# Attention and expert layer on one core: exponentials turned by way of HBM instead of on TensorE, scores ahead of values, and the order of the last scatters

## The chip, the cores and the metric

The kernel runs on one core of one Trainium2 chip. The core has TensorE (PE in the profile; its weight loads are PEld), VectorE (DVE), ScalarE (ACT), GpSimd (POOL) and SyncE (SP), which work through queues of their own and wait for one another by semaphores. Transfers are issued from the queues of SP, ACT and POOL and are carried by 16 DMA engines. The metric is device time of one execution in microseconds, the median of several. All data is float32.

## What is computed

Eight sequences of 512 tokens with 256 features go through one pre-norm layer: causal attention with one head, and a mixture of eight experts (two per token) beside a shared expert. Cut to what matters:

```
x = x + attention(layernorm(x))          # softmax(q k^T / 16, causal) v
h = layernorm(x)
shared = (silu(h @ sg.T) * (h @ su.T)) @ sd.T
p = sigmoid(h @ router.T + bias);  top 2 of 8, weights normalised to sum 1
routed = sum over the two experts e of weight * ((silu(h @ g[e]) * (h @ u[e])) @ d[e])
out = x + shared + routed
```

## The kernel before

**Tiling.** A tile has 128 partitions. A sequence has NT = 4 row blocks of 128 tokens; features are ND = 2 chunks of 128; the hidden layer has NI = 4 chunks. The weights of q and k are folded into one matrix (`w_qk`), so the scores are (x w_qk) x^T and only q is projected.

**Stages.** First a loop over sequences (`for b in range(B)`, L576): attention, router, the scatter of normalised tokens into rows by expert (`rows_h` in HBM), and half of the shared expert of an earlier sequence at a time. Then the routed experts in tiles of 256 or 128 rows (L821, results scattered to `rows_y`), and last the sums with the remaining shared work.

**One turn of the loop.** For each row block i, `scores` (L394) multiplies q by x^T (L399), adds the causal mask (L403), takes the row maximum (L405) and writes the exponentials to `ex` (L408). `attend` (L415) has PE transpose the i+1 squares of `ex` against an identity (L419), ScalarE copy them from PSUM to `exT` (L421), and PE multiply by the values (L426); VectorE adds the result to x (L429, the *residual sum* `summed`), takes mean and variance (L163, L164), GpSimd raises the variance to -1/2 (`rstd`, L170), and VectorE normalises to `hn` (L316). The scores of the next row block are issued ahead of the current block's values. During the last row block, q of the next sequence is projected (`project_q`, L375); then come its first scores and its values (`project_v`, L387, copied by VectorE at L391).

**Turning by way of HBM.** Normalised x of the sequences from 2 on and half of `hn` already go another way: SP writes them to HBM (L355), four transfers read them back so that each 32 partitions hold what a 32x32 transpose needs (L359), and VectorE transposes blocks of 32x32 (L364). The other half of `hn` is transposed on PE (L331).

**The rest of a turn.** `chosen` (L649) yields the transposes, the router product (L445), and the choice of two experts on VectorE, which ends in `run`, running counts by expert (L485). `places_of` (L490) turns counts into row numbers `at` with two small matmuls (L494, L495); it is called as `placed()` halfway through the shared expert's down product (`midway`, L546). `shared_beside` (L514) does the gate/up products (L528), the hidden product (L541, L544, marked `hid`) and the down product (L551). `dispatch` (L507) scatters a row block of `hn` with two indirect transfers on GpSimd (L509), spread over the row blocks of the next turn (L636).

**Order.** Instructions are written in program order, and a scheduler fixes each engine's queue at build time, taking what it reckons ready first. `tc.issue_after(x)` puts the instructions of a block behind x in the queue of x's own engine, and of that engine alone. `marks` keeps instructions for this. A pool's `bufs` is the number of buffers for a name; a writer waits until the oldest is free. PSUM has four buffers for scores, values and gate/up (`ps_m`), two for attention and down products (`ps_o`).

**The expert tiles.** How many single tiles are needed depends on the tokens. Tiles up to `SURE` are unconditional (L821), later ones are nested in conditions on a count read at run time (`go_on`, L844).

Of the kernel before, what the change touches and what calls it, by code (L numbers as in the profile page):

```python
# [26 lines left out]
def kernel(  # L27
# [37 lines left out]
    SURE = MEAN - 2  # L65
# [10 lines left out]
    VIA = [b for b in range(1, B) if b != B - 2]  # L76
    RS = 1.0 / D ** 0.5
# [15 lines left out]
    hn_d = {b: dram.tile([S // 2, D], F32, tag=f"hnd{b}", name=f"hnd{b}") for b in VIA}  # L93
    xn_d = {b: dram.tile([S, D], F32, tag=f"xnd{b}", name=f"xnd{b}") for b in range(2, B)}
# [172 lines left out]
    with ExitStack() as first, ExitStack() as inner:  # L267
# [66 lines left out]
        def first_norm(xb, step=NT):  # L334
            mv = small.tile([P, NT, 2], F32, tag="mv", name="mv")
            rstd = small.tile([P, NT], F32, tag="rstd", name="rstd")
            for c in range(NT):
                stats_of(mv, xb[:, c, :], c)
                if c % step == step - 1:
                    rstd_of(rstd[:, c + 1 - step : c + 1], mv[:, c + 1 - step : c + 1, :])  # L340
            rows = work.tile([P, NT, D], F32, tag="xn", name="xn")
# [9 lines left out]
        def sent_to_blocks(via, rows):  # L351
# [6 lines left out]
            for a in range(P // Q):  # L358
                nc.sync.dma_start(out=blocks[ts(a, Q)], in_=via[:, ts(a, L)].rearrange("(s i) l -> i s l", i=Q))  # L359
            return blocks  # L360
# [21 lines left out]
        def project_v(xT):  # L382
            v = work.tile([P, NT, D], F32, tag="v", name="v")
            for c in range(NT):
# [6 lines left out]
                nc.vector.tensor_copy(v[:, c, :], pm)  # L391
            return v

        def scores(i, qT, xT):  # L394
# [11 lines left out]
            ex = work.tile([P, S], F32, tag="ex", name="ex")  # L406
            tot = small.tile([P, 1], F32, tag="tot", name="tot")
            nc.scalar.activation(ex[:, :n], sc[:, :n], AF.Exp, bias=top, accum_out=tot)  # L408
# [6 lines left out]
        def attend(xb, i, ex, inv, v, mv, rstd, hn, meanwhile=None):  # L415
            n = (i + 1) * P
            pt = ps_t.tile([P, S], F32, tag="t", name="pt")
            for j in range(i + 1):
                nc.tensor.transpose(pt[:, ts(j, P)], ex[:, ts(j, P)], ident)  # L419
            exT = work.tile([P, S], F32, tag="exT", name="exT")  # L420
            marks["exT"] = nc.scalar.copy(exT[:, :n], pt[:, :n]).ins  # L421
# [3 lines left out]
            for j in range(i + 1):  # L425
# [3 lines left out]
            summed = nc.vector.scalar_tensor_tensor(  # L429
                out=xb[:, i, :], in0=av, scalar=inv, in1=xb[:, i, :], op0=ALU.mult, op1=ALU.add  # L430
            )
# [58 lines left out]
        def places_of(b, mask):  # L490
# [8 lines left out]
            for r in range(TOP):  # L499
# [4 lines left out]
                nc.vector.tensor_copy(at[:, r, :], slot)  # L504
# [9 lines left out]
        def shared_beside(b, half, hT, midway=None, early=None, steps=(), halfway=None):  # L514
# [8 lines left out]
            for m in range(NI):  # L523
# [20 lines left out]
                marks["hid"] = nc.vector.tensor_tensor(out=hid[:, m, :], in0=pg[:, 1, :], in1=sg, op=ALU.mult).ins  # L544
            for j in range(n // P):
# [15 lines left out]
        rows, normed = first_norm(xb, step=1)  # L561
# [13 lines left out]
        sc, sent, to_send, placed = scores(0, qT, xT), None, [], None  # L575
        for b in range(B):  # L576
            xb, ahead_T = total[b], None
            if b == 0:
                with tc.issue_after(normed):
                    rows, normed = first_norm(total[1])  # L580
                    ahead_T = turned_by_array(rows)
                with tc.issue_after(normed):
                    rows, _ = first_norm(total[2])
                blocks[2] = sent_to_blocks(xn_d[2], rows)
            elif b + 1 < B:
                ahead_T = work.tile([P, ND, S], F32, tag="xT", name="xT")
                turn_squares(ahead_T, blocks[b + 1], 0)
# [3 lines left out]
            if b and b + 2 < B:  # L591
                with tc.issue_after(marks["run"]):
                    rows, _ = first_norm(total[b + 2])
                blocks[b + 2] = sent_to_blocks(xn_d[b + 2], rows)
# [9 lines left out]
            for i in range(NT):  # L604


                if i + 1 < NT:
                    with nullcontext() if i or not b else tc.issue_after(marks["routed"]):
                        ahead = scores(i + 1, qT, xT)
                elif b + 1 < B:  # L610
# [3 lines left out]
                    xb, i, *sc, v, mv, rstd, hn, rest if i == NT - 1 and ahead_T is not None else None  # L614
                )
                sc = ahead
                if b in VIA and i == NT // 2:
                    halves = sent_to_blocks(hn_d[b], hn[:, : NT // 2, :D])
                if i == 0 and b + 1 in blocks:
# [379 lines left out]
```

## Time and profile before

| | us |
|---|---|
| median of 3 runs | 692.43 (691.06 to 693.13) |
| profiled execution | 694.9 |
| its span | 693.1 |
| PE busy | 675.8 |
| VectorE busy | 299.7 |
| ScalarE busy | 155.1 |
| GpSimd busy | 159.2 |
| one turn of the loop (109.53 to 138.78) | 29.25 |

The span runs from the first to the last instruction of the profiled execution; the execution's own time has 1.8 us around it. In the span the loop over sequences ends at about 257, routed experts begin at 277, and the closing sums at 628. Matmul ends are modelled, and a matmul of float32 appears as two records. In rows with an arrow, what stands left of it is written and what stands right is read; xN is the number of instructions; after a bar stand busy time and the mean of one in ns. A bracket in a timeline gives the idle time before an instruction and what ended it.

### The profile page before, as it was taken

The numbers are of one execution on the slowest core, as the hardware profiler recorded it, in microseconds if no ns is written. First come the engines' busy times: TensorE is split into PE (matmuls) and PEld (weight loads), VectorE is DVE, ScalarE is ACT, GpSimd is POOL, SyncE is SP. The second block draws the span as 40 slices with busy tenths as digits, with TensorE's granted clock in tenths as the row PEclk, the third lists the DMA queues.
The fourth block names the chain that finished last, engine by engine and source line by source line (L and its number), as shares of the span: only waits on it lengthen the run. The fifth ranks groups of instructions, "written<-read, shape, count | busy, mean of one in ns | idle before, by whom it ended". The sixth has DMA issues, their size and how long they took to land.

```text
span 693.1 us, 10478 instructions
## 1 busy us (share of the span) xinstructions
PE 675.8 (98%) x3258; PEld 550.6 (79%) x3258; DVE 299.7 (43%) x1009; ACT 155.1 (22%) x364; POOL 159.2 (23%) x210
## 2 busy tenths in 40 slices
PE   6999999999999799999999999999999999998998
PEld 5687776878777678888888888888888899994556
DVE  4667768677686565212212211222222112222665
ACT  2423233232333212221111111111111112111120
POOL 3106153351523540012112112112112111121000
PEclk9999999999999999999999999999999999999999
DMA  7775052241501263976555445435534447823875
GB/s 231 214 262 168 29 141 75 79 130 54 183 21 71 92 180 62 314 214 204 167 156 174 160 123 175 161 122 175 164 111 166 155 156 205 260 96 130 246 232 176
DMA packets 112794, 108.00 MB, mean 156 GB/s; under 512 B 72448, under 2 KB 92800, under 8 KB 112736
## 3 DMA queue, kind: packets, MB, share of 16 engines
q1 hardware_dynamic: 93536, 46.51, 24.9%
q10 hardware_dynamic: 12912, 43.53, 18.5%
q0 software_dynamic: 6288, 17.24, 7.0%
q8 instruction: 29, 0.48, 0.3%
q14 instruction: 29, 0.24, 0.1%
HBM read 77.55 MB, written 29.70 MB: 155 GB/s over the span
## 4 chain that ended last, share of the span: by engine, by line
PE 95%; DVE 3%; issue 1%; DMA 1%; ACT 1%; POOL 0%; SPq 0%; ACTq 0%
PE pg L771 17%; PE pu L771 17%; PE po L794 17%; PE pg L528 9%; PE av L426 5%; PE sc L399 5%; PE po L551 5%; PE pm L387 4%; PE pm L375 3%; PE pg L882 3%; PE po L941 3%; PE pu L882 3%; PE pt L419 1%; PE lT L445 1%; PE pt L331 1%
## 5 line engine op out<-in xcount | busy, mean ns | idle before, releaser
L757 DVE TENSOR_TENSOR hidp<-pu,sgt 128x512 f32<-128x512 f32 x56 | 38.6, 690 | 207.6 <-PE pu L771 192.1
L800 POOL DMA_INDIRECT rows_y<-y,to x56 | 53.5, 955 | 271.0 <-ACT y L799 147.3
L771 PE MATMUL pg<-hTt,w 128*128 128x256 f32 x448 | 105.9, 379 | 0.0
L771 PE MATMUL pu<-hTt,w 128*128 128x256 f32 x448 | 105.8, 379 | 0.0
L794 PE MATMUL po<-w_down,hidp 128*128 x448 | 101.3, 379 | 0.0
L771 PEld LDWEIGHTS pg<-hTt,w 128*128 128x128 f32 x448 | 85.0, 190 | 11.7 <-ACT sgt L756 0.2
L771 PEld LDWEIGHTS pu<-hTt,w 128*128 128x128 f32 x448 | 85.1, 190 | 11.6
L794 PEld LDWEIGHTS po<-w_down,hidp 128*128 128x128 f32 x448 | 85.0, 190 | 11.5
L528 PE MATMUL pg<-hT,w_sh 128*128 128x256 f32 x320 | 74.6, 382 | 0.2 <-ACT hT L332 0.2
L509 POOL DMA_INDIRECT rows_h<-hn,at x64 | 64.7, 1010 | 25.1 <-issue 16.1
L756 ACT ACTIVATE sgt<-pg 128x512 f32<-128x512 f32 x67 | 39.9, 597 | 122.2 <-PE pg L771 115.7
L528 PEld LDWEIGHTS pg<-hT,w_sh 128*128 128x128 f32 x320 | 58.9, 190 | 9.3 <-issue 1.4
L799 ACT COPY y<-po 128x256 f32<-128x256 f32 x67 | 24.9, 372 | 157.8 <-PE po L794 94.7
L170 POOL TENSOR_TENSOR rstd<-var,minus_half 128x1 f32<-128x1 f32 (+1 forms) x43 | 27.6, 645 | 136.2 <-DVE var L169 135.1
L399 PE MATMUL sc<-xT,qT 128*128 128x128 f32 (+3 forms) x128 | 42.8, 438 | 0.0
L426 PEld LDWEIGHTS av<-v,exT 128*128 128x128 f32 x160 | 29.1, 189 | 16.3 <-ACT exT L421 8.5
L426 PE MATMUL av<-v,exT 128*128 128x256 f32 x160 | 40.8, 386 | 0.0
L551 PE MATMUL po<-w_sh,hid 128*128 128x256 f32 x160 | 38.7, 380 | 2.1 <-DVE first L220 1.3
L551 PEld LDWEIGHTS po<-w_sh,hid 128*128 128x128 f32 x160 | 30.0, 190 | 7.1 <-DVE first L220 1.7
L375 PE MATMUL pm<-xT,w_qk 128*128 128x512 f32 x64 | 31.1, 593 | 0.0
L163 DVE BATCH_NORM_STATS2 bnst<-total 128x6 f32<-128x256 f32 x64 | 26.2, 412 | 7.5 <-DMA total<-in_x_dram 7.5
L387 PE MATMUL pm<-wv_sb,xT 128*128 128x256 f32 x128 | 29.1, 380 | 0.2 <-ACT xT L332 0.2
(150 smaller groups left out, 749.6 us busy)
## 6 DMA issues: line engine op xcount, KB each, us to landing
w<-in_gate_w_dram ACTq DMA_DIRECT2D x41, 512.0 KB
w<-in_up_w_dram ACTq DMA_DIRECT2D x41, 512.0 KB
yl<-rows_y SPq DMA_DIRECT2D x32, 256.0 KB
h<-rows_h SPq DMA_DIRECT2D x112, 64.0 KB
w_down<-in_down_w_dram SPq DMA_DIRECT2D x8, 512.0 KB
out_dram<-total SPq DMA_DIRECT2D x32, 128.0 KB
total<-in_x_dram SPq DMA_DIRECT2D x7, 512.0 KB
xnd<-xn SPq DMA_DIRECT2D x6, 512.0 KB
```

The lines of the kernel that those rows point to most:

```text
L375: nc.tensor.matmul(pm, lhsT=w_qk[:, k, ts(m, P)], rhs=xT[:, k, :], start=(k == 0), stop=(k == ND - 1),)
L387: nc.tensor.matmul(pm, lhsT=xT[:, k, ts(c, P)], rhs=wv_sb[:, k, :], start=(k == 0), stop=(k == ND - 1),)
L399: nc.tensor.matmul(sc[:, :n], lhsT=qT[:, k, ts(i, P)], rhs=xT[:, k, :n], start=(k == 0), stop=(k == ND - 1),)
L426: mixed = nc.tensor.matmul(av, lhsT=exT[:, ts(j, P)], rhs=v[:, j, :], start=(j == 0), stop=(j == i))
L509: lands(nc.gpsimd.indirect_dma_start(out=rows_h[:, :], out_offset=bass.IndirectOffsetOnAxis(ap=at[:, r, c : c + 1], axis=0), in_=hn[:, c, ...
L528: mm = nc.tensor.matmul(pg[:, w, :], lhsT=w_sh[:, ds(w * gu + k * I + m * P, P)], rhs=hT[:, k, at], start=(k == 0), stop=(k == ND - 1),)
L551: nc.tensor.matmul(po, lhsT=hid[:, m, ts(j, P)], rhs=w_sh[:, ds(2 * gu + m * D, D)], start=(m == 0), stop=(m == NI - 1),)
L756: nc.scalar.activation(sg, pg, AF.Silu)
L771: nc.tensor.matmul(dst[:, m, :], lhsT=w[:, i, k, ts(m0 + m, P)], rhs=hT[:, ts(k, n * P)], start=(k == 0), stop=(k == ND - 1),)
L794: nc.tensor.matmul(po, lhsT=hid[:, m, ts(j, P)], rhs=w_down[:, ds(w + m * D, D)], start=(m == 0), stop=(m == NI - 1),)
L800: nc.gpsimd.indirect_dma_start(out=rows_y[:, :], out_offset=bass.IndirectOffsetOnAxis(ap=to[:, j : j + 1], axis=0), in_=y, in_offset=None,)
L882: nc.tensor.matmul(dst, lhsT=w_sh[:, ds(off + k * I + m * P, P)], rhs=hT[:, k, :], start=(k == 0), stop=(k == ND - 1),)
```

## The change

For sequences 1 to 6 (`SENT`) the exponentials are no longer transposed on PE. All four row blocks' scores are computed together at the end of the turn before, ahead of the values. The exponentials of row blocks 0 to 2 stand side by side in one tile of 6 squares, those of row block 3 in one of 4. Each tile is written to HBM and read back by four transfers in runs of 32 elements (128 bytes), and VectorE turns it with one block transpose behind the hidden product (`behind`). `attend` then takes its part of the turned tile. Sequences 0 and 7 keep the transposes on PE.

With it: the values are copied by ScalarE for those sequences; `first_norm` is split into statistics (`first_stats`, at the end of the turn) and normalisation (`midway`), for sequence b+3 in turn b where it was b+2; q of the next sequence is projected in two halves, before row blocks 0 and 2; the shared result is added (`added`) at the turn's end; loads of x and down weights, and the write of `hT`, queue behind the new gathers on SP; `placed()` on VectorE stands behind the new transposes. In the last sequence, row block 2 dispatches one pair of scatters instead of two, and row block 3 the other three. `SURE` grows by one, so one more expert tile is unconditional.

```diff
-    SURE = MEAN - 2
+    SURE = MEAN - 1
+    SENT = range(1, B - 1)
+    BLOCKS = NT * (NT - 1) // 2, NT
...
-        def first_norm(xb, step=NT):
+        def first_stats(xb, step=NT):
             mv = small.tile([P, NT, 2], F32, tag="mv", name="mv")
...
+            return xb, mv, rstd
+
+        def first_norm(xb, mv, rstd):
             rows = work.tile([P, NT, D], F32, tag="xn", name="xn")
...
-        def project_v(xT):
+        def project_v(xT, copy=nc.vector.tensor_copy):
...
-                nc.vector.tensor_copy(v[:, c, :], pm)
+                copy(v[:, c, :], pm)
...
+        def part(of, i):
+            return of[1] if i == NT - 1 else of[0][:, ds(i * (i + 1) // 2 * P, (i + 1) * P)]
+
+        def sent_to_squares(via, ex):
+            if "blocks" in marks:
+                with tc.issue_after(marks["blocks"]):
+                    nc.sync.dma_start(out=via, in_=ex)
+            else:
+                nc.sync.dma_start(out=via, in_=ex)
+            n = via.shape[1] // P
+            blocks = work.tile([P, n * P], F32, tag=f"squares{n}", name="squares", bufs=1)
+            for a in range(P // Q):
+                marks["sent"] = nc.sync.dma_start(
+                    out=blocks[ts(a, Q)].rearrange("j (t s i) -> j t s i", t=n, i=Q),
+                    in_=via[:, :].rearrange("(s j) (t a i) -> a j t s i", j=Q, t=n, i=Q)[a],
+                ).ins
+            return blocks
+
+        def turn_exponentials(blocks):
+            exT = []
+            for of in blocks:
+                exT.append(work.tile(list(of.shape), F32, tag=f"exTs{of.shape[1]}", name="exTs", bufs=1))
+                marks["turned"] = nc.vector.transpose(out=exT[-1], in_=of).ins
+            return exT
+
-        def scores(i, qT, xT):
+        def scores(i, qT, xT, into=None):
...
-            ex = work.tile([P, S], F32, tag="ex", name="ex")
+            ex = work.tile([P, S], F32, tag="ex", name="ex")[:, :n] if into is None else part(into, i)
...
-        def attend(xb, i, ex, inv, v, mv, rstd, hn, meanwhile=None):
+        def attend(xb, i, ex, inv, v, mv, rstd, hn, meanwhile=None, exT=None):
...
+            if exT is None:
...
+            else:
+                exT = part(exT, i)
...
-            summed = nc.vector.scalar_tensor_tensor(
+            with tc.issue_after(marks["turned"]) if "turned" in marks else nullcontext():
+                summed = nc.vector.scalar_tensor_tensor(
...
-        def shared_beside(b, half, hT, midway=None, early=None, steps=(), halfway=None):
+        def shared_beside(b, half, hT, midway=None, behind=None, early=None, steps=(), halfway=None):
...
+            if behind is not None:
+                behind()
             for j in range(n // P):
...
-                turn_squares(ahead_T, blocks[b + 1], 0)
+                with tc.issue_after(marks["half"]) if b - 1 in VIA else nullcontext():
+                    turn_squares(ahead_T, blocks[b + 1], 0)
+                if b in SENT:
+                    with tc.issue_after(marks["run"]):
+                        turn_squares(ahead_T, blocks[b + 1], 1)
+                    queued = marks["sent"]
...
-            if b and b + 2 < B:
-                with tc.issue_after(marks["run"]):
-                    rows, _ = first_norm(total[b + 2])
-                blocks[b + 2] = sent_to_blocks(xn_d[b + 2], rows)
...
+                if b in SENT:
+                    sc = exs[i]
+                    if i % 2 == 0:
+                        with tc.issue_after(mixed) if i else nullcontext():
+                            qT = project_q(ahead_T, range(i // 2 * ND // 2, (i // 2 + 1) * ND // 2), qT if i else None)
-                if i + 1 < NT:
+                elif i + 1 < NT:
...
-                for _ in range(-(-len(to_send) // (NT - i))):
+                for _ in range(-(-len(to_send) // (NT - i)) if b + 1 < B or i == NT - 1 else min(1, len(to_send))):
...
-                    sc = scores(0, qT, ahead_T)
-                    v = project_v(ahead_T)
+                    if b + 1 in SENT:
+                        ex = [work.tile([P, n * P], F32, tag=f"exs{n}", name="exs", bufs=1) for n in BLOCKS]
+                        exs = [scores(i, qT, ahead_T, ex) for i in range(NT - 1)]
+                        squares = [sent_to_squares(ex_d[b + 1][0], ex[0])]
+                        exs.append(scores(NT - 1, qT, ahead_T, ex))
+                        squares.append(sent_to_squares(ex_d[b + 1][1], ex[1]))
+                        v = project_v(ahead_T, nc.scalar.copy)
+                    else:
+                        sc = scores(0, qT, ahead_T)
+                        v = project_v(ahead_T)
...
+            if added is not None:
+                with tc.issue_after(normed.ins):
+                    added()
+                added = None
...
+            if b + 3 < B:
+                with tc.issue_after(marks["half"] if b in VIA else normed.ins):
+                    coming = first_stats(total[b + 3])
...
-                nc.sync.dma_start(out=hT_d[b], in_=hT)
+                with tc.issue_after(marks["sent"]):
+                    nc.sync.dma_start(out=hT_d[b], in_=hT)
...
+                    def behind():
+                        nonlocal exT
+                        with tc.issue_after(marks["hid"]):
+                            exT = turn_exponentials(squares)
+
+                    def midway():
+                        with tc.issue_after(marks["turned"]):
+                            placed()
+                        if b + 3 < B:
+                            with tc.issue_after(marks["placed"]):
+                                rows, _ = first_norm(*coming)
+                            with tc.issue_after(marks["sent"]):
+                                blocks[b + 3], _ = sent_to_blocks(xn_d[b + 3], rows)
```

## The prediction

> **What bounds the kernel now.** I read the page first: busy shares and the chain that ended last.
>
> ```profile
> PE 675.8 (98%) x3258; PEld 550.6 (79%) x3258; DVE 299.7 (43%) x1009; ACT 155.1 (22%) x364; POOL 159.2 (23%) x210
> ...
> PE 95%; DVE 3%; issue 1%; DMA 1%; ACT 1%; POOL 0%; SPq 0%; ACTq 0%
> ```
>
> TensorE (PE) is busy 98% of 693.1 us and carries 95% of the chain. A share is an average, so next I took the view by stretches over one turn of the loop over sequences (the marks at 109.53 and 138.78 are the same matmul one turn apart) and over the loop's end:
>
> ```profile
> 109.53:138.78 29.25, 29.23 (x145) 22.24 (x144) 21.99 (x91) 8.48 (x23) 11.43 (x13) 1.00 0.33 91
> ...
> 227.00:257.00 30.00, 25.11 (x130) 20.20 (x128) 19.17 (x98) 4.89 (x14) 16.58 (x18) 1.00 0.41 125
> ```
>
> After the stretch stand its length and the busy time of PE, weight loads, VectorE, ScalarE, GpSimd, then clock and DMA share. In a turn PE is busy 29.23 of 29.25 us at clock 1.00: only less PE work shortens it, and VectorE has 7.3 us to spare. From 227 to 257, where the last sequence has little beside it, PE idles 4.9 us. The chain in time gives the transposes' price on PE:
>
> ```profile
> 112.98 0.22 PE pt L419 x2
> ...
> 117.50 0.42 PE pt L419 x3
> ...
> 120.12 0.44 PE pt L419 x4
> ...
> 129.37 0.11 PE pt L419
> ```
>
> Ten transposes of exponentials take 0.22+0.42+0.44+0.11 = 1.19 us of each turn; nothing else fills those slots.
>
> **Removed: 60 transposes and 24 copies.** In sequences 1 to 6 the transposes go: 6 x 1.19 = 7.1 us, all on the path. Their PSUM copies on ScalarE (586+482+373+262 ns by the group rows, 1.7 us a turn) go too; four copies of V (4 x 385 ns, the row of an ACT copy of 128x256 from PSUM being 372 to 385) come there from VectorE. ScalarE is busy 8.5 of 29 us, so both cost nothing; without that cover it would be 0.2 us either way. VectorE loses 4 x 413 ns = 1.65 us of V copies and gains the two block transposes. The rows are 442 ns for 256 columns and 703 for 512, so 768 take some 0.96: 0.96+0.70 = 1.66 us. VectorE's total stays.
>
> **Added: the way through HBM.** I count from T, the end of a sequence's last attention-times-values matmul (L426 x8; 123.28 in the turn above). PE's new order after T, each piece at its length in the chain: scores 0.45+0.86+1.29+1.72 = 4.32; values 3.46, to 7.8; transposes of hn 0.46; gate/up 1.73, router 0.57, gate/up 1.73, 0.11, gate/up 3.46, to 15.8; shared down 1.73, positions 0.36, shared down 1.73, to 19.7; first half of the next q 1.72, to 21.4. Only then does PE want the first turned exponentials. Then av(0), av(1), half q: 0.43+0.86+1.72, so av(2) starts at 24.4. On SyncE's queue:
>
> ```profile
> 114.34 0.38 SPq L355 DMA_DIRECT2D xnd<-xn  x1
> 117.27 2.13 SPq L359 DMA_DIRECT2D blocks<-xnd  x4
> 120.99 0.38 SPq L355 DMA_DIRECT2D hnd<-hn  x1
> 123.94 1.85 SPq L359 DMA_DIRECT2D blocks<-hnd  x4
> ```
>
> A write and the wait for its landing take 2.93 to 2.95 us, four gathers 1.85 to 2.13 us to issue. The new writes are put behind the gather of hn: its write leaves after row block 2, at about T-0.8, its gathers are issued T+2.1 to T+4.0. The first new write needs the exponentials of row block 2: scores end T+2.6, then 0.29+0.55 on VectorE and 0.58+0.19 on ScalarE, behind up to 1.6 us of the residual sum and its statistics: T+4.4 to T+6; I take T+5. It lands at T+7.9; the second write fits in between, since SyncE would only wait. The gathers bring 6x512 + 4x512 = 5120 runs of 128 bytes. No row has such runs. The nearest are runs of 256 bytes:
>
> ```profile
> DMA  0000691999998899999799996000093037995537
> ```
>
> This is the DMA busy strip of 117 to 127 us, quarter microseconds a digit. The 2048 runs of blocks<-xnd keep it at 9 from 118.75 to about 123.0, the hn write inside: 2.1 ns a run. The 1024 runs of blocks<-hnd, with scatters beside them, take 124.25 to 127: 2.7 ns. If bytes alone counted, 128 bytes would cost half, 1.05 ns. I take 2.1, since the row counts runs, not bytes, and keep 1.05 and 2.7 as ends. Data starts some 0.8 us after the issue, so all has landed at 7.9+0.8+10.8 = T+19.5 (ends T+14.1 and T+22.5).
>
> What waits for it: on VectorE both block transposes stand behind the last product of the hidden layer (1.34 us after the last gate/up in this trace: T+17.2), and behind them the places (1.2 us) and the next residual sum (0.48). The third attention tile needs the PSUM buffer that this sum frees. So the second block may land at 24.4-0.5-1.2-0.7 = T+22.0 with no cost: 2.5 us to spare at my value, 0.5 us short a turn (3 us in all) at the dear end. The first block has 3072 of the 5120 runs, lands at T+15.2 and is wanted at T+20.4. The places come 5 us later after T than now, but the scatters that use them start in the next turn, after its first rstd, so they stay covered.
>
> The Trainium skill, "DMA: Bandwidth & Descriptors", Specifications, speaks against this: under 512 bytes a descriptor is a read-modify-write and loses line rate. If that doubled a run to 4.2 ns (an estimate), all would land near T+30 and the kernel would lose some 40 us. The strip, whose runs are under 512 bytes too, is why I don't take it. The skill's "VectorE: DVE Perf Modes", Rules for kernel authors, also prefers TensorE for a 128x128 transpose if PSUM can take it. By the rows a square costs PE 0.12 us and VectorE 0.17, so taken alone that rule holds; by it the sum would be zero or a loss. Here PE is full and VectorE is not.
>
> **Moved: scores, sums, statistics, loads.** Scores 1 to 3 and their VectorE work (3.1 us with score 0), the addition of shared results (0.66) and the statistics of a later x (4 x (0.41+0.17)+0.16 = 2.5) now stand in T to T+17. With the sum and norms (2.0), two turns (1.4), hidden products (3.4) and routing (4.0) that is some 17 us of single durations; by the stretch view VectorE's instructions overlap (27.5 us of durations in 21.99 busy), so 14 us of 17.2. It fits with 3 us over. Before, scores of the next sequence filled the PE between shared down and positions (136.84, 0.43 and 138.27, 0.51); that filler is gone, and routing needs some 6 us from its logits to `run` while PE has 5.2 us before positions unless the second shared down goes first. I bound the new PE waits: none, or 0.8 us a turn (6 less 5.2); below zero too, since the chain holds 0.2 us of waiting at positions now (0.41 where 0.22 is enough). I take +0.2. The loads of x and of down weights now queue behind the gathers; x is wanted some 20 us after that (T+13 to the next T+5), cover enough: the row above lands 0.5 MB in 2.9 us. If that cover went, VectorE would stand on it for about as long, once a turn. The normalised x and the stored hT pass SyncE's queue behind the gathers as well; the one is used a turn later, the other after the loop.
>
> **Order of the last scatters.** GpSimd, last sequence:
>
> ```profile
> 227.34 0.55 POOL L170 TENSOR_TENSOR rstd<-var,minus_half 128x1 f32<-128x1 f32 x1 [2.59 <-DVE var L169]
> 228.06 1.04 POOL L509 DMA_INDIRECT rows_h<-hn,at  x1 [0.18 <-issue]
> 229.40 0.96 POOL L509 DMA_INDIRECT rows_h<-hn,at  x1 [0.30 <-issue]
> 230.66 0.96 POOL L509 DMA_INDIRECT rows_h<-hn,at  x1 [0.30 <-issue]
> 231.93 0.96 POOL L509 DMA_INDIRECT rows_h<-hn,at  x1 [0.30 <-issue]
> 232.91 0.57 POOL L170 TENSOR_TENSOR rstd<-var,minus_half 128x1 f32<-128x1 f32 x1
> ```
>
> The last rstd has its input at 230.71 and waits for four scatters. With two ahead it starts at about 230.8, 2.1 us sooner, and VectorE's normalisation with it. PE's own idle there is 1.29 us (transposes of hn at 233.99), and the next gate/up took 2.16 where 0.86 is enough, as VectorE was held: 1.3 to 2.6; I take 2.0. Six scatters after it end at 231.5+6x1.28 = 239.2, against 238.6, and the next begin only at 247.
>
> **One more certain tile.** Here 39 expert tiles run (28 pairs and 11 singles by the rows). Tile 38 leaves the conditional part. PE shows no gap on entering it; the 1.32 us of issue at 623.75 is the jump past unused tiles, and it stays, one level shallower. I take 0, between -0.3 and +0.3.
>
> **Sum.** A turn: -1.19+0.2 = -1.0; six turns -6.0; scatters -2.0; conditional 0: -8.0. The profiled execution took 694.9 (span 693.1 and 1.8 around it), 2.5 above the median; 694.9 - 8.0 = 686.9 there, and the same step off the median of 692.43 gives 684.4.
>
> **Rivals.** (1) VectorE becomes the brake in T to T+17: its 82% there holds up the maxima, so the exponentials, the value tiles' PSUM and the positions, at the 0.8 us bound. Against it: 3 us over. Six turns give 6 x 0.4 = 2.4, scatters the low 1.3: 688.7. (2) The gathers are late. Past T+22.0 a turn grows by each microsecond; it passes the gain at (8.0+2.1)/6 = 1.7 us late, T+23.7, which is 2.9 ns a run. For it: the run is shorter than any in the trace and 2.7 was seen; against: 2.7 was beside scatters. At 3.2 ns they land at T+25.1, 3.1 us late: 684.4 + 18.6 = 703. (3) It does not do what it says: the scheduler, which orders each engine's queue at build time, puts the second shared down after positions and half q after av(0), and PE waits what it saved: 692.
>
> **How the numbers follow.** Main case 0.61, rival (1) 0.18, (2) 0.16, (3) 0.05. The measurement tells 0.3%, 2.1 us. Faster: 0.61+0.18 less a little of (1), 0.78; same 0.05; slower 0.17. Low end: no new waits and the present extras in a turn gone (a turn of bare pieces is 27.4 us, 1.8 less), so 6 x 1.8 and 2.6 off: 679; high end: up to case (3), 693, which leaves out (2).
>
> **What would show it.** Right: a turn of 28.0 to 28.3 us; L419 at 20; block transposes of 768 and 512 columns done before av(0); no VectorE idle released by the new gathers; rstd of the last sequence near 231. Wrong: VectorE waiting for the gathers, PE idle before av or positions, a gather of over 14 us.

## The result: slower by 2.6%, and the profile after

The changed kernel took 710.28 us (708.35 to 711.72) against 692.78 for the kernel before beside it: a ratio of 1.0256, with an interval of 1.0237 to 1.0275. The forecast was 684.4, and its range ended at 693. The profiled execution has a span of 709.9 us, 16.8 above before. The page of the changed kernel, busy shares and the chain that ended last:

```profile
PE 679.4 (96%) x3198; PEld 549.2 (77%) x3198; DVE 299.4 (42%) x997; ACT 152.9 (22%) x364; POOL 160.4 (23%) x210
...
PE 80%; DVE 9%; POOL 6%; issue 2%; DMA 1%; ACT 1%; SPq 0%; DVEq 0%; ACTq 0%; POOLq 0%
```

PE has lost its 60 transposes and now carries only 80% of the chain, where it carried 95%. VectorE has 9% and GpSimd 6%; before they had 3 and 0. In this profile lines have moved: the matmul that marks a turn is L538 (before L495), values L398, attention times values L468, mask L442, maximum L444, exponentials L447, the residual sum L472, the normalisation L322, rstd L176, scatters L552, the block transposes of exponentials L430. The marks show where the 16.8 us arose:

| stretch | before | after | difference |
|---|---|---|---|
| start to the first mark of the loop | 50.14 | 53.94 | +3.8 |
| first to sixth mark, five turns | 146.22 | 166.31 | +20.1 |
| sixth mark to the first expert tile | 80.50 | 74.84 | -5.7 |
| first expert tile to the end | 416.24 | 414.81 | -1.4 |

So the five turns cost 4.0 us more each, where 1.0 less was forecast, and all that was gained lies behind them (most of it isn't the change's, as e4's profile shows further down). The view by stretches of the changed kernel, the first and the fourth turn (length, then busy time of PE, weight loads, VectorE, ScalarE, GpSimd, clock, DMA share):

```profile
54.31:89.07 34.76, 31.51 (x135) 23.04 (x135) 22.15 (x90) 8.14 (x23) 11.69 (x13) 0.90 0.56 145
155.69:188.22 32.53, 28.69 (x134) 21.30 (x135) 22.23 (x89) 8.04 (x23) 11.66 (x13) 1.00 0.54 147
```

Before, PE was busy 29.23 of 29.25 us. Now it idles 3.84 us of the fourth turn. VectorE's total of 22.2 us is what it was (22.0): it has not become the brake by its amount of work. In the first turn the granted clock is 0.90 as well, and matmuls there take longer. What PE waits for is in its timeline of the fourth turn; a bracket gives the idle time before an instruction and what ended it:

```profile
162.09 3.19 PE L468 MATMUL av<-v,exTs 128*128 128x256 f32 x14
165.11 4.48 PE L438 MATMUL sc<-xT,qT 128*128 128x128 f32 x16
171.53 1.99 PE L398 MATMUL pm<-wv_sb,xT 128*128 128x256 f32 x8 [1.94 <-issue]
175.24 1.99 PE L398 MATMUL pm<-wv_sb,xT 128*128 128x256 f32 x8 [1.72 <-ACT exs L447]
```

Scores of all four row blocks end at 169.6; the values then wait 1.94 and 1.72 us. The four scores hold all four PSUM buffers for scores, values and gate/up, so a value tile cannot start before an exponential has read its score. The exponentials wait for the maxima, which stand in VectorE's queue:

```profile
166.25 0.41 DVE L322 TENSOR_SCALAR hn<-total,mv,rstd 128x256 f32<-128x256 f32 x1 [1.47 <-POOL rstd L176]
...
169.47 0.41 DVE L322 TENSOR_SCALAR hn<-total,mv,rstd 128x256 f32<-128x256 f32 x1 [1.67 <-POOL rstd L176]
...
170.14 0.28 DVE L442 TENSOR_TENSOR sc<-sc,causal 128x128 f32<-128x128 f32 x1
...
170.65 0.61 DVE L444 TENSOR_REDUCE top<-sc 128x1 f32<-128x128 f32 x2
172.68 0.41 DVE L322 TENSOR_SCALAR hn<-total,mv,rstd 128x256 f32<-128x256 f32 x1 [1.41 <-POOL rstd L176]
...
173.08 0.28 DVE L442 TENSOR_TENSOR sc<-sc,causal 128x128 f32<-128x128 f32 x1
```

The first score exists before 166, but its mask begins at 170.14, behind two normalisations that waited 1.47 and 1.67 us for rstd; the third row block's mask stands behind the last normalisation, which waited 1.41. Nothing in the data makes a mask wait for rstd: VectorE takes its queue in order. And rstd is late on GpSimd:

```profile
162.62 0.55 POOL L176 TENSOR_TENSOR rstd<-var,minus_half 128x1 f32<-128x1 f32 x1 [12.90 <-DVE hn L680]
163.33 1.04 POOL L552 DMA_INDIRECT rows_h<-hn,at  x1 [0.17 <-issue]
164.67 0.96 POOL L552 DMA_INDIRECT rows_h<-hn,at  x1 [0.30 <-issue]
165.66 0.56 POOL L176 TENSOR_TENSOR rstd<-var,minus_half 128x1 f32<-128x1 f32 x1
166.41 1.17 POOL L552 DMA_INDIRECT rows_h<-hn,at  x1 [0.19 <-issue]
167.88 0.96 POOL L552 DMA_INDIRECT rows_h<-hn,at  x1 [0.30 <-issue]
168.87 0.57 POOL L176 TENSOR_TENSOR rstd<-var,minus_half 128x1 f32<-128x1 f32 x1
...
172.08 0.57 POOL L176 TENSOR_TENSOR rstd<-var,minus_half 128x1 f32<-128x1 f32 x1
```

Between two rstds lies a pair of scatters; rstd and pair together take 3.0 to 3.2 us, so the fourth rstd cannot start earlier than 9.5 us after the first. Before the change GpSimd had the same work at the same pace (rstd at 115.78, 118.81, 121.88, 125.20), but PE's attention took 12.2 us then, from the start of the first row block's values product to the end of the last (111.10 to 123.28), with scores, transposes and q in between. Now it takes 6.2 (159.07 to 165.28). The scatters no longer fit into it.

### The profile page after: what moved, and what is told of

Read it like the earlier page. It is cut to its first block, busy times and chain, and to the rows that moved or that the text cites. A ratio compares the mean times of both kernels' runs of the same rounds, so it can differ in the third digit from the quotient of the medians.

```text
span 709.9 us, 10399 instructions
## 1 busy us (share of the span) xinstructions
PE 679.4 (96%) x3198; PEld 549.2 (77%) x3198; DVE 299.4 (42%) x997; ACT 152.9 (22%) x364; POOL 160.4 (23%) x210
## 4 chain that ended last, share of the span: by engine, by line
PE 80%; DVE 9%; POOL 6%; issue 2%; DMA 1%; ACT 1%; SPq 0%; DVEq 0%; ACTq 0%; POOLq 0%
PE pu L855 16%; PE pg L855 16%; PE po L878 16%; PE pg L571 7%; POOL rows_h L552 4%; PE po L596 3%; PE pg L966 3%; PE po L1025 3%; PE pu L966 3%; PE pm L398 3%; PE pm L386 2%; PE av L468 2%; PE sc L438 2%; POOL rstd L176 2%; DVE sg L584 1%
## 5 line engine op out<-in xcount | busy, mean ns | idle before, releaser
L552 POOL DMA_INDIRECT rows_h<-hn,at x64 | 65.6, 1025 | 21.5 <-issue 16.1
L176 POOL TENSOR_TENSOR rstd<-var,minus_half 128x1 f32<-128x1 f32 (+1 forms) x43 | 27.4, 639 | 158.3 <-DVE var L175 87.8
L398 PE MATMUL pm<-wv_sb,xT 128*128 128x256 f32 x128 | 38.3, 454 | 16.3 <-issue 9.9
L398 PEld LDWEIGHTS pm<-wv_sb,xT 128*128 128x128 f32 x128 | 27.4, 223 | 28.5 <-issue 15.2
L438 PE MATMUL sc<-xT,qT 128*128 128x128 f32 (+3 forms) x128 | 37.4, 434 | 0.0
L468 PEld LDWEIGHTS av<-v,exTs 128*128 128x128 f32 x120 | 22.8, 190 | 8.2 <-issue 5.5
```

The source lines that it names most:

```text
L176: return nc.gpsimd.tensor_tensor(out=rstd, in0=var, in1=minus_half[:, :n], op=ALU.pow).ins
L398: nc.tensor.matmul(pm, lhsT=xT[:, k, ts(c, P)], rhs=wv_sb[:, k, :], start=(k == 0), stop=(k == ND - 1),)
L438: nc.tensor.matmul(sc[:, :n], lhsT=qT[:, k, ts(i, P)], rhs=xT[:, k, :n], start=(k == 0), stop=(k == ND - 1),)
L552: lands(nc.gpsimd.indirect_dma_start(out=rows_h[:, :], out_offset=bass.IndirectOffsetOnAxis(ap=at[:, r, c : c + 1], axis=0), in_=hn[:, c, ...
```

## Theories and experiments

Theory G: GpSimd's pairs of scatters between the rstds delay VectorE's normalisations, VectorE's order passes the delay on to the maxima, and the full PSUM passes it on to PE. Rival H: the way through HBM with its VectorE transposes and queueing on SyncE is the cause. Theory C, later: what is left without G is a chain through VectorE. The kernels of one series ran on one chip, beside the kernel before. The changed kernel itself ran beside variants on the fourth chip alone; otherwise ratios are compared across chips:

| series | kernel before, us | ratios to it |
|---|---|---|
| recorded run | 692.78 | changed kernel 1.0256 |
| first chip | 691.14 | e1 1.0023, e2 1.0322, e3 0.9981, e4 1.0012 |
| second chip | 691.12 | e6 1.0014, e7 0.9979, e8 1.0148 |
| third chip | 695.22 | e9 1.0187, e10 1.0210, e7 1.0215 |
| fourth chip | 695.61 | changed kernel 1.0241, e1 1.0294, e7 1.0157, e8 1.0404 |
| fifth chip | 692.41 | e11 0.9984, e6 1.0012, e3 0.9985 |

### All scatters behind the fourth rstd (e1)

```diff
-for _ in range(-(-len(to_send) // (NT - i)) if b + 1 < B or i == NT - 1 else min(1, len(to_send))):
+for _ in range(len(to_send) if i == NT - 1 else min(1, len(to_send)) if b + 1 == B or b not in SENT else 0):
```

> The changed kernel, but in sequences 1 to 6 all eight scatters stand behind the fourth rstd on GpSimd instead of two behind each. Theory G (six scatters stand between the first and the fourth rstd of a turn; VectorE stands on the normalisations that need these rstd, with the masks and maxima of the next scores behind them in its queue, so PE waits before the values): the waits of 1.9 and 1.7 us before the values go, a turn falls from 32.4 to some 28.8 us, the two turns with the lower clock from 34.5 to 28.8 too, the clock stays at 1.00, and the time falls by 26 us to 684 (680 to 688). Theory H (the way through HBM, that is the gathers or the block transposes, makes the turns long): the scatters' order changes nothing, 708 to 712.

Measured on the first chip: 692.97 us, 1.0023 (1.0011 to 1.0035), 17 us under the recorded run of the changed kernel, far under H's 708 but above G's 680 to 688. The first five turns take 28.5 to 29.6 us and the waits at the values are gone. Not all of G's 26 us came back: PE busy falls to 28.49 of 29.60 us, and the router product now waits for the transposed hn, which comes late by a chain through VectorE and HBM. From the views by stretches and of PE's timeline of this kernel:

```profile
112.24:141.84 29.60, 28.49 (x133) 21.37 (x133) 22.01 (x89) 8.05 (x24) 11.03 (x13) 1.00 0.61 168
```

```profile
126.38 3.88 PE L398 MATMUL pm<-wv_sb,xT 128*128 128x256 f32 x16
...
133.39 0.65 PE L488 MATMUL lT<-hT,r_sb 128*32 128x128 f32 x16 [0.93 <-DVE hT L375]
```

### The same order without the way through HBM (e2), and with the scatters moved as well (e8)

```diff
-squares = [sent_to_squares(ex_d[b + 1][0], ex[0])]
...
-squares.append(sent_to_squares(ex_d[b + 1][1], ex[1]))
...
-xb, i, *sc, v, mv, rstd, hn, rest, exT if b in SENT else None
+xb, i, *sc, v, mv, rstd, hn, rest, None
...
-added = shared_beside(*waiting.pop(0), midway=midway, behind=behind, early=choice, steps=((0, 1), (1, 1)))
+added = shared_beside(*waiting.pop(0), midway=midway, early=choice, steps=((0, 1), (1, 1)))
```

Beside these lines, what was queued behind the gathers no longer is, and `placed()` stands behind the hidden product.

> The changed kernel, but sequences 1 to 6 transpose their exponentials on PE again: no write to HBM, no gathers, no block transposes; scores stay together ahead of the values, scatters as in the changed kernel. Theory G: the way through HBM is not the cause, PE gets 1.19 us of transposes back in a turn while it waits on GpSimd's chain anyway, so 709 to 717. Theory H: the cause is gone and the time comes back to the kernel before less what the end gained, 686 to 692.

e2 gave 711.42 us, 1.0322 (1.0272 to 1.0371), on the same chip as e1: with transposes on PE and no new transfers the loss is there, so H falls. Its values wait 0.92 and 1.57 us for the exponentials, as in the changed kernel. e8 is e2 with e1's order of scatters:

> The kernel with all scatters behind the fourth rstd, but exponentials transposed on PE, without the way through HBM. If PE's time bounds a turn, the ten transposes cost their 1.19 us each turn: 700. If the chain of theory C bounds it, PE has room for most of them: 692 to 696.

On the second chip 701.29 us, 1.0148 (1.0131 to 1.0165). The first two chips' times of the kernel before agree to 0.02 us, and neither shows the ScalarE waits described further on, so their ratios can be set side by side: the pairs between the rstds cost 1.0322 - 1.0148, 12 us, even where PE has its transposes, and e8 against e1, 1.0148 - 1.0023, puts the way through HBM 8.6 us ahead of PE's transposes. Of that, by the profiled spans, 4.6 us lie ahead of the first expert tile (282.29 against 277.71; the five turns are 151.3 against 145.7, 1.1 us a turn, about what ten transposes cost) and 3.4 behind it, where e8 has an issue gap of 1.98 us at the jump past unused tiles and e1 none.

### All scatters behind the first rstd (e5)

In the loop of e1, `i == 0` in the place of `i == NT - 1`: the suspected wait made longer.

> The changed kernel, but in sequences 1 to 6 all eight scatters stand behind the first rstd: eight between the first and the fourth instead of six. Theory G: two scatters more, 2 x 1.24 us, in every turn's chain, so a turn goes from 32.4 to some 34.9 us and the time to 725 (720 to 732). If only the number of scatters in a turn counts and not their place: 710.

One execution took 740.48 us, beside 691.12. Direction and place are G's, the amount is larger: PE's timeline shows one wait of 7.62 us a turn at the values, after which they run at half speed (6.78 us for 16 matmuls, where e1 has 3.88), and the clock over the turn is 0.87:

```profile
150.07 6.78 PE L398 MATMUL pm<-wv_sb,xT 128*128 128x256 f32 x16 [7.62 <-ACT exs L447]
```

### Pairs left in place, masks and maxima ahead of two normalisations (e6)

```diff
+with tc.issue_after(marks["topped"]) if b + 1 in SENT else nullcontext():
+    if b + 1 in SENT:
+        normalize(hn[:, NT - 2, :D], xb, NT - 2, mv, rstd)
     normed = normalize(hn[:, NT - 1, :D], xb, NT - 1, mv, rstd)
```

`marks["topped"]` is the last maximum; `attend` leaves the third row block's normalisation out for these turns.

> The changed kernel with its scatters in place, but on VectorE the normalisations of row blocks 2 and 3 stand behind the masks and maxima of the next sequence's scores instead of ahead of or among them. Theory G in its narrow form (it is VectorE's queue order that passes GpSimd's delay on to PE, since no score needs hn): the waits of 1.9 and 1.7 us before the values go, what is left is hn coming late by way of HBM for the router; a turn of some 29 to 30.4 us, 692 to 699. If GpSimd's delay reaches PE by data anyway: 708 to 712.

Measured 692.68 us, 1.0014 (0.9995 to 1.0034). GpSimd is as late as in the changed kernel (rstds at 119.33, 122.37, 125.44 and 128.52 in one turn), but only hn waits for it, and PE goes from the scores, which end at 126.4, to the values without a wait:

```profile
121.90 4.48 PE L438 MATMUL sc<-xT,qT 128*128 128x128 f32 x16
126.21 3.83 PE L398 MATMUL pm<-wv_sb,xT 128*128 128x256 f32 x16
```

The middle link, VectorE's order, decides. On the fifth chip:

> Scatters in pairs behind each rstd as in the changed kernel, with the masks and maxima ahead of the normalisations on VectorE: no row of eight in the loop. If the row makes ScalarE stand, this keeps its 1.0014 on any chip; if the way through HBM or the order of scores does, it goes to 1.02 on a chip that shows the stall.

It took 693.24 us there, 1.0012 (0.9996 to 1.0027). That is some 16 us under the changed kernel's 1.024 to 1.026 (measured on other chips), on two chips, by a change in VectorE's queue alone.

### Places and normalised x ahead of the first residual sum (e7)

e1, and VectorE's queue turned once more: in the changed kernel the sum of a turn's first row block stands ahead of the places and of four normalisations of a later x, and its variance behind them (159.71 to 162.32 in the fourth turn).

```diff
 placed()
+marks["turned"] = marks["placed"]
...
-rows, _ = first_norm(*coming)
+rows, marks["turned"] = first_norm(*coming)
```

> The kernel with all scatters behind the fourth rstd, and on VectorE the places and the normalisation of the later x stand ahead of the first residual sum, in a gap of 2.06 us in which VectorE waits for the first attention tile, instead of between that sum and its variance. Theory C (with the scatters out of the way a turn of 29.2 us is a chain through VectorE: residual sum, variance, rstd, hn by way of HBM, router, counts, positions, and the next attention): the chain loses about 2 us, PE's own 27.4 to 28 us takes over: 684 to 687. If PE's work or the gathers bound the turn at 29.2: 691 to 694.

On the second chip 689.55 us, 0.9979 (0.9969 to 0.9989). The view by stretches of one turn:

```profile
109.80:138.13 28.33, 28.15 (x133) 21.46 (x133) 22.63 (x89) 8.16 (x24) 10.97 (x13) 1.00 0.65 174
```

With both orders mended a turn takes 28.33 us: this is what the prediction wanted of the change (28.0 to 28.3), and PE idles 0.18. C holds for the turn. The time is above the expected 684 to 687. In the last sequence PE waits 4.51 us behind VectorE, whose copy into hn stands 5.04 us for the scatters that still read that buffer, and matmuls after it run at half speed; whether that is all that is missing was the question for e9.

### A third buffer, and other chips (e9, e10, e7 again)

e9 is e7 with `bufs=3` for hn; e10 is e9 with `SURE = MEAN - 2` as before.

> The preceding variant (all eight scatters behind the fourth rstd, places and normalised x ahead of the first residual sum, 0.9979 of the kernel before) with a third buffer for hn. There VectorE's copy of the places into hn in the last sequence waited 5.04 us for the scatters that read the same buffer, and PE waited 4.51 us behind it. Theory W: that wait is what held back the last sequence; with a third buffer it is gone and the time falls by 3 to 5 us to 684 to 687 (ratio 0.989 to 0.994). Rival K: the last sequence is bound by something else that is late by the same time, GpSimd's row of eight scatters ahead of its rstds above all; then 688.5 to 690.5, as without the buffer.

> The same with one expert tile fewer certain, as in the kernel before. By the run of that edit alone (+0.8 us) this gives 0.8 us less than with the tile; if the tile costs nothing here, as its gap at the jump was gone in the changed kernel, the same time to 0.3 us; if it gains there, 1.3 us more.

> The variant without the third buffer again, on the same chip, for the comparison: 689.5 (0.9979 of the kernel before) as in its first run, within 0.7 us.

All missed. On this third chip e7 took 709.72 us against 695.22 (1.0215), e9 707.92 and e10 710.17; their intervals overlap, so neither the buffer nor the tile can be read from them (the copy's wait is gone from e9's profile, as meant, but PE then waits 3.23 us for ScalarE there; so what held back the last sequence in e7 stays open). ScalarE is what differs. From its timeline in one turn of e7 on that chip, and PE behind it:

```profile
136.09 0.59 ACT L338 COPY hT<-pt 128x512 f32<-128x512 f32 x1 [0.23 <-PE pt L337]
141.80 0.38 ACT L582 ACTIVATE sg<-pg 128x256 f32<-128x256 f32 x1 [5.13 <-remote]
```

```profile
135.74 1.89 PE L571 MATMUL pg<-hT,w_sh 128*128 128x256 f32 x8
...
142.40 0.33 PE L496 MATMUL pl<-ident,logits 128*128 128x128 f32 x1 [2.26 <-ACT logits L493]
```

The activation's input, the first gate/up product, is complete at 137.6. It starts at 141.80, and the trace shows nothing that it waited for; the last of eight scatters in a row was issued until 140.2. On the second chip the same program starts it within 1.2 us of the instruction before.

### The changed kernel, e1, e7 and e8 on one chip

> The changed kernel itself, beside the variants on one chip. In the last series the variant with the places ahead of the residual sum took 709.7 us where its first run, on another chip, took 689.6; its trace shows ScalarE standing 4 to 5 us once a turn ahead of the first activation of the hidden layer (ScalarE sg, released by nothing in this trace) and PE's router product behind it, and the kernel before took 695.2 there against 691.1. So part of what I read as the cost of the change could be that chip's. Theory G (scatters between the rstds, whatever the chip): the changed kernel is 15 us or more above the variant with all scatters behind the fourth rstd on this same chip. Rival X (the chip): the changed kernel and the variant are within 5 us.

> All eight scatters behind the fourth rstd. Theory G: 15 us or more under the changed kernel on this chip, 1.002 of the kernel before where ScalarE doesn't stand. Where it does stand, six turns by 3 to 4 us come on top (1.03), and then the stall needs the eight scatters beside the gathers if the changed kernel's own trace shows none.

> Places and normalised x ahead of the first residual sum as well. Where ScalarE doesn't stand: 0.998 of the kernel before; where it does: 1.02, as in its second run. 3 to 4 us under the run with the scatters alone in either case, if the two effects add.

> Scatters behind the fourth rstd, but exponentials transposed on PE, no way through HBM and no gathers of 128-byte runs. If ScalarE's stall comes from those gathers, this run has none on any chip and stays at 1.015 of the kernel before; if it comes from the eight scatters in a row, it stands here too, some 1.03 on a chip that shows it.

The fourth chip: changed kernel 712.52 us, 1.0241 (1.0216 to 1.0267); e1 716.06; e7 706.67; e8 723.51. G's 15 us between e1 and the changed kernel did not show here: they are 3.5 us apart the other way, which was rival X's sign. X's cause is not borne out all the same, since the changed kernel has 1.0241 here for 1.0256 in the recorded run. e1's 1.03 came as expected; e7 is 9.4 us under it, not 3 to 4, and e8 is above its 1.03. ScalarE stands in e1, e7 and e8, which have eight scatters in a row, and not in the changed kernel's loop, which has pairs. e8 has no gathers of 128-byte runs, so these aren't needed for it. PE's waits for ScalarE's logits, in e1 on the first chip and then in e1 on the fourth, and last the changed kernel's waits at the values on the fourth (total us, times, longest):

```profile
PE pl L496 <- ACT logits L493: 0.4, 1, 0.4
```

```profile
PE pl L496 <- ACT logits L493: 15.3, 6, 3.3
```

```profile
PE pm L398 <- issue: 10.3, 6, 2.3
PE pm L398 <- ACT exs L447: 5.1, 4, 1.5
```

So on this chip moving the scatters takes G's waits away and puts others in their place.

### Four and four (e11), and the last scatters alone (e3)

e7, but in sequences 1 to 4 four scatters behind the fourth rstd and four behind the rstd of the coming x:

```diff
+for _ in range(len(to_send)):
+    with tc.issue_after(marks["coming"]):
+        dispatch(*sent, to_send.pop(0))
```

> The variant with places and normalised x ahead of the first residual sum, but in sequences 1 to 4 only four scatters stand behind the fourth rstd and four behind the later rstd of the coming x, some 12 us on. On one pair of chips that variant took 0.998 of the kernel before, on another pair 1.016 to 1.022, where ScalarE stood 3 to 5 us a turn during the row of eight scatters. If the stall needs a long row, four turns lose it: on a chip that shows it 8 to 16 us less than with eight (0.995 to 1.005), on the other chips no change (0.998). If the stall comes with any scatters beside ScalarE's work in this part of the turn, it stays (1.016 to 1.022), in two shorter pieces.

On the fifth chip 692.02 us, 0.9984 (0.9969 to 0.9999). This profile holds both cases in one execution, four turns with four and four and then one with eight. Its stretches, the fourth and the fifth turn, and ScalarE's timeline in each:

```profile
139.86:168.21 28.35, 28.15 (x133) 21.46 (x133) 22.65 (x89) 7.95 (x23) 11.07 (x13) 1.00 0.66 170
168.21:199.63 31.42, 28.54 (x134) 21.44 (x134) 21.10 (x80) 8.29 (x24) 9.94 (x12) 1.00 0.68 196
```

```profile
159.85 0.38 ACT L582 ACTIVATE sg<-pg 128x256 f32<-128x256 f32 x1 [1.08 <-PE pg L571]
...
191.65 0.38 ACT L582 ACTIVATE sg<-pg 128x256 f32<-128x256 f32 x1 [3.89 <-PE pg L571]
```

With four in a row the activation starts after 1.08 us, with eight after 3.89 (its input was there at 188.8; the eighth scatter was issued until 191.3), and the turn is 3.1 us longer. The fifth turn also lacks the work on a later x, but on the third chip e7's turns that have it stand too. That the long row goes with the stall on such a chip is shown; by what it holds ScalarE up, and why not on the first two chips, is open.

e3 is the kernel before with one line of the change, the order of the last scatters:

```diff
-for _ in range(-(-len(to_send) // (NT - i))):
+for _ in range(-(-len(to_send) // (NT - i)) if b + 1 < B or i == NT - 1 else min(1, len(to_send))):
```

> The kernel before with only the order of the last scatters changed. The prediction has -2.0 us (690.5). The trace of the changed kernel has 43.6 us from the end of the last sequence's attention to the first expert tile where the kernel before had 47.9: if that is all from this order, -4.3 us (688.3).

> The kernel before with the new order of the last scatters alone: 0.998 on any chip, 1.3 us less, since it has no row of eight in the loop and no way through HBM for exponentials.

689.68 us on the first chip, 0.9981 (0.997 to 0.9992), and 691.46 on the fifth, 0.9985 (0.9974 to 0.9996): 1.3 and 1.0 us less. This one line gains on both of its chips. e7 (on the second chip) and e11 gain about as much, and e7 not everywhere.

### One more certain tile alone (e4)

The kernel before with `SURE = MEAN - 1`.

> The kernel before with only SURE one greater. The prediction has 0 (692.4). The trace of the changed kernel shows no issue gap of 1.32 us after the last tiles' down product: if this edit removes it, -1.3 us (691.2).

691.82 us, 1.0012 (1.0002 to 1.0022): 0.8 us more. The gap at the jump is there, in PE's timeline 2.18 us long, and the four matmuls after it take 3.78 us where the kernel before, after a gap of 1.32, has 1.98:

```profile
622.10 2.73 PE L794 MATMUL po<-w_down,khid 128*128 x8 [2.18 <-issue]
625.42 3.78 PE L882 MATMUL pg<-hTl,w_sh 128*128 128x512 f32 x4 [0.59 <-ACT y L799]
```

## Why the prediction was wrong, step by step

**Removed: right, about the size.** In a turn PE is busy 28.15 us in e7 and 28.49 in e1, against 29.23 before: 0.7 to 1.1 us less, where 1.19 was forecast. e8 against e1 gives 1.1 us a turn; of the 8.6 us in all, 3.4 are the jump past unused tiles and not transposes. ScalarE's and VectorE's totals stay, as said.

**The way through HBM: in time, and cheaper than priced.** In the fourth turn attention ends at T = 165.28. The writes leave at 175.21, T+9.9 in the place of T+5, since the exponentials are late. The gathers start 2.6 us later:

```profile
175.21 1.43 SPq L414 DMA_DIRECT2D exd<-exs  x2
177.79 6.70 SPq L420 DMA_DIRECT2D squares<-exd  x8
```

The busy strip of the DMA engines from 174 to 188, 0.35 us a digit:

```profile
DMA  5790088999910019556998679938110079999799
```

The packets of 128 bytes, 5120 of them, run from 179.1 to 185.8: the last gather's come after the dip at 184.5, as the counts for 179 to 186 and for 184.5 to 186 show.

```profile
DMA packets 5282, 0.81 MB, mean 115 GB/s; under 512 B 5248, under 2 KB 5248, under 8 KB 5281
```

```profile
DMA packets 599, 0.21 MB, mean 137 GB/s; under 512 B 566, under 2 KB 566, under 8 KB 599
```

That is 1.3 ns a run, 6.6 us in all; the prediction took 2.1 ns and 10.8 us. The eight issues take 6.7 us, so their pace may set it, which isn't shown. All is there at T+20.5, within the T+22.0 that the prediction allowed, although the gathers began 4.6 us later than it had them. Both block transposes (188.54, 1.56 us) follow VectorE's work without a wait. The rule of the Trainium skill that it set against the strip ("DMA: Bandwidth & Descriptors", Specifications: read-modify-write below 512 bytes) did not show as the doubling that was priced: 1.3 ns for 128 bytes here, 2.1 for 256 bytes there. The slower rival, late gathers, was the wrong one.

**Moved: the step that failed.** "I bound the new PE waits: none, or 0.8 us a turn ... I take +0.2": the trace shows 3.84 us of PE idle in the fourth turn. The step counted VectorE's work from T to T+17 as a sum, 14 of 17.2 us, and concluded "it fits with 3 us over". The amount of work was as counted (22.2 us a turn after 22.0), but VectorE got only 10.2 us done between T and T+17.2, because of its order: masks and maxima stand behind normalisations that wait for GpSimd. "TensorE: Matmul & The Clock Gate" of the Trainium skill (Part 1, Architectural detail) says that VectorE takes its queue strictly first in, first out; the rows above show it, with 4.55 us of waiting for rstd ahead of masks that need none. GpSimd's queue, its rstds and eight scatters in 12.7 us (162.62 to 175.27), wasn't counted for the six turns at all, although the same mechanism, an rstd behind scatters, was priced for the last sequence. The step also left out that four scores at once fill the PSUM that the values need. And it didn't ask what shortening PE's attention from 12.2 to 6.2 us does to work that ran in its shadow: the scatters had been "covered" by a stretch that the change itself cut in half.

**Rival 1** named the place (maxima, exponentials, the value tiles' PSUM) but took its price from the same bound, 0.8 us, and so stayed on the faster side. The range's high end, 693, was rival 3's; 703, for late gathers, was left out of it, and no rival had GpSimd in it.

**Order of the last scatters: right mechanism, over-sized.** Forecast -2.0 (1.3 to 2.6), measured -1.3 and -1.0. Part of the idle time in the kernel before's recorded profile was none of the order's: ScalarE's logits there start at 238.23, with 2.29 us of idle time before them, during eight scatters with one rstd between them. In e4, with the same order on the first chip, that gap is 0.18 us, and the stretch from the sixth mark to the first expert tile is 76.4 us for the recorded 80.5. So some 4 of the 5.7 us that this stretch seemed to gain belong to that execution of the kernel before. The two rows, e4's second:

```profile
238.23 0.27 ACT L450 COPY logits<-lT 128x128 f32<-128x128 f32 x1 [2.29 <-PE pg L528]
```

```profile
236.37 0.27 ACT L450 COPY logits<-lT 128x128 f32<-128x128 f32 x1 [0.18 <-PE lT L445]
```

So the stall of the later chips was already in the trace that I predicted from, and I took it for part of the kernel.

**One more certain tile.** Forecast 0 (-0.3 to +0.3), measured +0.8 alone (interval 0.1 to 1.5). The gap at the jump, forecast to stay, is gone in the changed kernel, in e1 and in e10, which has one certain tile fewer, but stays in e2, e3, e4 and e8; so it goes with the block transposes of exponentials and not with the tile, and by what isn't settled.

## What to carry to other kernels

Before a change shortens the bounding engine's stretch, list every queue that ran in the shadow of that stretch, in order, with its length; here eight scatters and four rstds needed 12.7 us and were left with 6.2. An engine with spare time is not a free one: ask which instruction at the head of its queue waits for whom, and what stands behind it without needing to. If a small operation on one engine feeds a queue on another, keep long issues away from it, but not all in one row before looking at a second chip.

## What the runs showed of the hardware

**ScalarE and rows of scatters.** On the third, fourth and fifth chip, and in the last sequence of both recorded profiles (the kernel before and the changed one), ScalarE stood 1 to 5 us with its input complete, during eight indirect scatters in a row (one rstd among them at the kernel before's logits) or up to 2 us behind them; on the first two chips it didn't. Shorter rows go with shorter stands. The activation behind the last sequence's logits, beside six scatters in a row in most variants, starts 0.04 us after its input in every profile of the first two chips, and 0.5 to 1.2 us after it in all others. With four in a row (e11) up to 0.8 us was seen, with pairs nothing above 0.5. The ratios of e1 and e8 are 0.027 and 0.026 higher on the fourth chip than on the first two; in e1 PE's waits for the logits, 15.3 us, are most of that. A variant measured on one chip alone would have been called a gain (e7, 0.9979) or a loss (e7, 1.0215).

**The clock after short waits.** Some waits of about 2 us were followed by matmuls at half speed: in the changed kernel's first turn, after 2.23 and 0.84 us (eight value matmuls 3.78 us for 1.99), and in e4 after 2.18. After 1.94 and 1.72 us in the fourth turn they weren't. Length alone doesn't decide: 1.88 us was enough in the changed kernel's second turn, and after 2.50 us in e7 and 3.23 us in e9, both on the third chip, the clock stayed at 1.00. From the first mark on, it fell after every wait above 3.3 us. "TensorE: Matmul & The Clock Gate" (Why this matters for your kernels) asks for no idle gaps above about 3 us; here shorter ones were at times enough. A wait thus can cost more than its length, as e5 shows most.
